# A first convolution by seven products of blocks, and the normed last batch finished by accumulating loads

## The chip, the core and the metric

The kernel runs on one core of a Trainium2 chip. The core has a matrix engine (TensorE, PE in the profile; PEld is its weight load), VectorE (DVE), ScalarE (ACT), GpSimd (POOL), and SyncE (SP), which here does nothing but issue DMA transfers. The metric is the time of one execution on the device in microseconds, the median of several. All arrays are float32.

## What is computed

The reference takes x of shape (4, 1024, 32, 32), so B = 4 batches of C = 1024 channels and N = 1024 tokens, through two layers.

```
layer 0 (attention, per batch; tokens x channels):
  q, k, v = split(x @ w_qkv.T + b_qkv)          # 16 heads of 64
  q, k = rmsnorm(rope(q)), rmsnorm(rope(k))     # over all 1024 channels
  ctx = softmax(q k^T / 8) v
  x1 = rmsnorm(ctx @ w_proj.T) * norm_out_w + x
layer 1 (bottleneck, over all four batches together):
  h1 = relu(bn(conv1x1(x1, w1) + b1))           # 1024 -> 256 channels
  h2 = relu(bn(conv3x3(h1, w2) + b2))           # 256 -> 256
  h3 = bn(conv1x1(h2, w3) + b3)                 # 256 -> 1024
  out = relu(x1 + softplus(residual_scale) * h3)
```

A batch norm (bn) needs the mean and variance of a channel over all four batches, so no part of h1 can be used before the first convolution is done for every batch. The change lies in that convolution and in the end of layer 0 for the last batch.

## The kernel before

`program` (line 86) goes through the batches in order. For each one it projects q, k and v, turns and norms q and k, does the attention head pair by head pair, and projects the result (`qk_proj` with the tag "y", line 1087). The tiles are 128 channels (partitions) by 512 tokens, half a batch; N = 1024 tokens are two such halves (`half`, line 180), 1024 channels are NT = 8 tiles.

The big projections already use products of blocks. A matrix product in which both operands are cut in 2 x 2 blocks is done with seven block products instead of eight, after Strassen in Winograd's form: operand blocks are added and subtracted first (VectorE: `sums` at line 271 for the rows, `operands` at line 224 for the weights, where the four sums are called S1 to S4), and the products are added up in two PSUM banks, one of which is read out several times while it accumulates (`project`, lines 321 to 361). `project2` (line 432) does this on two levels for the later batches. The first convolution does not: `conv1` (line 847) accumulates eight matmuls (1024 input channels in eight tiles) for one of two blocks of 128 output channels and one half of the tokens. That is 4 x 8 = 32 matmuls of 128x512 a batch.

The result y of the last projection of a batch is scaled by the reciprocal root of its mean square. `inverse_rms` (line 657) sums squares over channels with a small matmul (`ss_y`, line 666), takes the root (ScalarE), the reciprocal (VectorE), stores that row to DRAM and broadcasts it to all partitions, both from GpSimd's queue (lines 676 and 677). For batches 0 to 2, `o_norm` then scales y and stores it to `x1d` in DRAM; the input x is added there later by accumulating DMA transfers (line 1037). For the last batch, `last_norm` (line 830) does it in 16 half tiles: VectorE scales, VectorE adds x, which was loaded into the tile `xr` (line 1098), and SP stores to `x1d` (line 837). y stays in SBUF, because the first convolution of batch 3 reads it from there.

After the last projection stand the first convolutions, from line 1094: batch 1 from `back[1]`, batch 2 from `back[2]`, batch 0 from `back[0]`, all read back from `x1d`, and batch 3 from y (line 1194). `back[1]` is read during the last projection (line 1080). `back[0]` takes the place of `back[1]` and so can only be loaded when batch 1 is done. Each result h goes through ScalarE (bias, PSUM to a temporary), VectorE (`bn_stats` for the batch norm) and SP (store to `h1d`). Batch 3 is last; when its first 128 channels are done, the batch norm is put together and the 3x3 convolution begins.

Order of the work: TensorE, GpSimd, VectorE and ScalarE run their instructions in the order in which the program records them (`manual_schedule`, lines 91 and 964). An instruction that waits holds up all that is recorded behind it on its engine. `product_done` (line 252) counts the products; with `after(n, step)` a step is recorded n products later, with `waiting` when the count allows. SP's queue is ordered by a planner when the kernel is built. SBUF is full: the temporaries (`temp`, four of 128x512), the large ones (`big_temp`, three), eight weight chunks (`chunk`) and the large tiles "v", "q", "x" and "k" are handed on from use to use, and a new user waits until the old one is done.

Of the kernel before, what the change touches and what calls it, by code (L numbers as in the profile page):

```python
# [12 lines left out]
AF = mybir.ActivationFunctionType  # L13
ALU = mybir.AluOpType
# [4 lines left out]
P = 128  # L19
B, C, H, W = 4, 1024, 32, 32  # L20
N = H * W
NT = C // P
HD = 64
NHP = C // (2 * HD)
CH = 512
NCH = N // CH
# [3 lines left out]
NPT = PL // P  # L30
# [31 lines left out]
NH = NT // 2  # L62
NG = NT // 2
QH = P // 4
SUMS = ("S2", "S1", "S3", "S4")
# [20 lines left out]
def program(ctx, tc, x, wblk, w2, w3, vecs, cos, sin, out, bad):  # L86


    nc = tc.nc
# [6 lines left out]
    x1d = dram.tile([NT, P, B * N], F32, name=f"x1d{u}")  # L96
    h1d = dram.tile([NPT, P, B * N], F32, name=f"h1d{u}")
# [13 lines left out]
    def col(name, i=0):  # L111
        return vec[:, COL[name] + i : COL[name] + i + 1]
# [30 lines left out]
    h1stats = const.tile([P, NPT, B * NCH, nc.vector.BN_STATS_DIM], F32, name="h1stats")  # L143
# [9 lines left out]
    with tc.tile_pool(name=f"st{u}", bufs=2) as st, ExitStack() as s:  # L153
# [25 lines left out]
        yt = {}  # L179
        half = [slice(c * CH, (c + 1) * CH) for c in range(NCH)]  # L180
# [17 lines left out]
        def bank(kind, name):  # L198
            pool, shape = psum[kind]
            return pool.tile(shape, F32, tag=kind, name=name)  # L200

        def temp(name):
            return tmp.tile([P, CH], F32, tag="tmp", name=name)

        def big_temp(name):
            return big.tile([P, N], F32, tag="big", name=name)
# [5 lines left out]
        def chunk(name):  # L212
            return wring.tile([P, NH, P], F32, tag="w", name=name)
# [28 lines left out]
        TT = 0.21  # L242
        later, waiting = [], deque()
# [5 lines left out]
        def after(n, step):  # L249
            later.append((pace["at"] + n, step))  # L250

        def product_done(share=1.0):
            pace["at"] += share
            pace["room"] = min(pace["room"] + share, 1.2)
            due = [s for at, s in later if at <= pace["at"]]
            later[:] = [(at, s) for at, s in later if at > pace["at"]]
            for step in due:
                step()
            while waiting and pace["room"] > 0 and not pace["hold"]:
                next_waiting()  # L260

        def next_waiting():
            cost, step = waiting.popleft()
            spend(cost)
            step()
# [561 lines left out]

            inverse_rms(total, eps_rms, 1.0 / C, f"y_{b}", then)

        def last_norm(b, total, ys, xr):  # L830


            def norm(f, at):
                y = ys[:, f, at]
                nc.vector.scalar_tensor_tensor(y, y, col("ow", f), total[:, at], ALU.mult, ALU.mult)
                nc.vector.tensor_tensor(y, y, xr[:, f, at], ALU.add)
                nc.sync.dma_start(x1d[f, :, b * N + at.start : b * N + at.stop], y)

            def then():
                waiting.extend([(2 * TT, lambda f=f, at=at: norm(f, at)) for at in half for f in range(NT)])  # L840

            inverse_rms(total, eps_rms, 1.0 / C, f"y_{b}", then)

        def conv1_weights(name):
            return [[block(W1, f, ih, f"c1_{name}_{f}_{ih}") for ih in range(2)] for f in range(NPT)]

        def conv1(b, f, c, w, ys, then=None):
            o = bank("o2", f"c1_{b}_{c}_{f}")
            for i in range(NT):
                ih, ii = divmod(i, NH)  # L850
                nc.tensor.matmul(  # L851
                    o, w[f][ih][:, ii, :], ys[:, i, half[c]], start=(i == 0), stop=(i == NT - 1)
                )
                if i == NH - 1:
                    product_done()
            h = temp(f"h1_{b}_{c}_{f}")
            nc.scalar.activation(h, o, AF.Identity, bias=col("b1", f))

            def stats():
                nc.vector.bn_stats(h1stats[:, f, b * NCH + c, :], h)  # L860
                nc.sync.dma_start(h1d[f, :, b * N + c * CH : b * N + (c + 1) * CH], h)
                if then is not None:
                    then()

            after(1, stats)
            product_done()

        def norm_of(stats, g, be, name):
# [48 lines left out]
        def read_back(b, rows=range(NT)):  # L917
            for i in rows:
                nc.sync.dma_start(back[b][:, i, :], x1d[i, :, b * N : (b + 1) * N])

        def x_tile(b):
            return xp.tile([P, NT, N], F32, tag="x", name=f"x_{b}")
# [4 lines left out]
        def v_room(name):  # L927
            return kv.tile([P, N // P, C], F32, tag="v", name=name)
# [47 lines left out]
        room = v_room("rq_0")  # L976
        for b in range(B):
# [69 lines left out]
            room = v_room(f"to_{b}")  # L1047
# [12 lines left out]
            if b + 1 < B:  # L1060
                xs[b + 1] = x_tile(b + 1)
                ts[b + 1] = t_tiles(b + 1)
                rows = (0, 1, 4, 5, 2, 3, 6, 7)
                for j in range(NT):

                    def load(b=b, i=rows[j]):
                        for c in range(NCH):
                            load_x(b + 1, c, (i,))

                    after(3 + 1.5 * j, load)  # L1070
                for i in range(0, NH, 2):

                    def queue(b=b, i=i):
                        waiting.append((7 * TT, lambda: sums(ts[b + 1], xs[b + 1], i)))

                    after(3 + 1.5 * (2 * i + 3) + 2, queue)
            else:
                back = {1: x_tile(b + 1)}
                for i in range(NT):
                    after(8 + 1.5 * i, lambda i=i: read_back(1, (i,)))  # L1080
            if b == 0:
                weight_parts([parts_of[WK][k] for k in (2, 3)], 6, 7, 4, pieces_of(room[:, 3 * NT // 4 :, :]))
            yt[b] = kp.tile([P, NT, N], F32, tag="k", name=f"y_{b}")
# [3 lines left out]
            ty = qk_proj(b, WP, q_all, tc_, None, yt[b], "y", None, two)  # L1087
            if b + 1 < B:
                o_norm(b, ty, yt[b])
            else:  # L1090
                xr = v_room("xr")
                last_norm(b, ty, yt[b], xr)

        back[2] = kv.tile([P, NT, N], F32, tag="q", name="back")
        read_back(2)
        w = conv1_weights("last")
        for i in range(NT):
            nc.sync.dma_start(xr[:, i, :], x[B - 1, i * P : (i + 1) * P, :])
        for b in (1, 2, 0):
            if b == 0:  # L1100
                back[0] = x_tile("back")
                read_back(0)
            for c in range(NCH):
                for f in range(NPT):
                    conv1(b, f, c, w, back[b])
        rest()
        if bad is not None:
            dt = temp("dens")
# [169 lines left out]
        for b in range(B):  # L1278
            steps = []
            if b + 1 < B:  # L1280
                steps = transform(b + 1, 0) + transform(b + 1, 1)
# [5 lines left out]
            for f in range(NPT):  # L1287
                for h in range(2):
# [14 lines left out]
                    steps = steps[4:]  # L1303
# [9 lines left out]
            if b == 0 and bad is not None:  # L1313
                o = ps.tile([P, CH], F32, tag="mm", name="fit")
# [20 lines left out]
        for f in range(NT):  # L1335
            if f > 0 and f + 2 < NT:
                load_x1(f + 2)
            stats = st.tile([P, B * NCH, nc.vector.BN_STATS_DIM], F32, tag="s3", name=f"s3_{f}")
# [5 lines left out]
            for i, k in order:  # L1344
                b, c = divmod(i, NCH)
                nc.tensor.matmul(  # L1346
                    os[i], w3t[k][f // NH][:, f % NH, :], h2[b, k][:, half[c]],
                    start=(k == 0), stop=(k == NPT - 1),
# [3 lines left out]
                h = h3s[f % 2][:, b, half[c]]  # L1352
# [89 lines left out]
```

## Time and profile before

| | |
|---|---|
| median of 3 runs | 2709.47 us (2709.33 to 2710.42) |
| the profiled execution | 2709.99 us, span 2708.2 us |
| TensorE busy in the span | 2669.3 us, 99% |
| VectorE, ScalarE, GpSimd busy | 2169.5, 1096.1 and 452.6 us |
| mean granted clock of TensorE | 0.995 |
| moved from and to HBM | 316.71 MB read, 96.78 MB written |

The span runs from the first to the last instruction; the execution's time has a little around it. Times inside the trace count from the start of the span. "Waits" of an engine are idle times and what ended them. The clock is the share of full speed that was granted to TensorE. A matmul of the source appears as two records[...]. Records overlap, so a matmul's cost is read from start to start.

### The profile page before, as it was taken

What the parts mean: (1) busy time and instruction counts of PE and PEld (TensorE: products, weight loads), DVE (VectorE), ACT (ScalarE), POOL (GpSimd) and SP (SyncE); (2) the same over time, 40 slices, a digit from 0 to 9 for tenths busy, and PEclk for the clock granted to TensorE, in tenths of its full rate; (3) what the DMA queues carried; (4) which work ended last, traced back from release to release, by engine and by line L of the source; (5) the groups of instructions that cost most, each with busy time, mean ns of one, the idle gap of its engine ahead of it and who ended that gap; (6) DMA issues with size and microseconds to landing.
All of it is one profiled execution on the core that took longest, in us unless ns stands there. A gap on an engine that the chain in (4) does not pass through costs nothing. (4 is left out here: it accounts for less than half of the span.)

```text
span 2708.2 us, 32563 instructions
## 1 busy us (share of the span) xinstructions
PE 2669.3 (99%) x11410; PEld 1659.0 (61%) x11410; DVE 2169.5 (80%) x2516; ACT 1096.1 (40%) x1520; POOL 452.6 (17%) x552
## 2 busy tenths in 40 slices
PE   9999999999999999999999999999999999999997
PEld 4448533488888333688886333888884335746843
DVE  4577899998887977888878877987888878646987
ACT  2222455523342555333343555233525553312266
POOL 2562222322011211100111211100111211000000
PEclk9999999999999999999999999999999999999999
DMA  7897755587677341456765420665783314662165
GB/s 272 317 306 214 230 154 165 167 269 246 197 203 213 62 92 32 148 152 222 188 189 144 88 54 17 214 205 173 189 233 79 75 36 132 196 240 86 63 227 209
DMA packets 245964, 453.54 MB, mean 167 GB/s; under 512 B 28384, under 2 KB 117264, under 8 KB 245792
## 3 DMA queue, kind: packets, MB, share of 16 engines
q1 hardware_dynamic: 203568, 310.72, 36.5%
q0 software_dynamic: 42224, 140.63, 19.6%
q8 instruction: 94, 1.54, 0.2%
q14 instruction: 78, 0.64, 0.1%
HBM read 316.71 MB, written 96.78 MB: 153 GB/s over the span
## 5 line engine op out<-in xcount | busy, mean ns | idle before, releaser
L768 DVE TENSOR_TENSOR den<-den,p 128x1024 f32<-128x1024 f32 x384 | 470.5, 1225 | 40.7 <-DVE den L768 0.9
L764 ACT ACTIVATE p<-sc 128x1024 f32<-128x1024 f32 x512 | 476.3, 1043 | 55.0 <-PE sc L757 54.8
L757 PE MATMUL sc<-q,k 64*128 64x512 f32 x2048 | 457.7, 596 | 0.0
L757 PEld LDWEIGHTS sc<-q,k 64*128 64x128 f32 x2048 | 189.9, 186 | 265.6 <-issue 121.2
L774 PE MATMUL cx<-p,to 128*64 128x512 f32 x1536 | 340.2, 595 | 0.0
L774 PEld LDWEIGHTS cx<-p,to 128*64 128x64 f32 x1536 | 106.0, 137 | 228.3 <-issue 228.3
L738 POOL TENSOR_SCALAR q<-q,vec 128x512 f32<-128x512 f32 x64 | 127.0, 1989 | 559.2 <-DVE q L737 559.2
L453 PE MATMUL p_v<-w_v,x 128*128 128x256 f32 x928 | 210.8, 380 | 1.3 <-DVE x L424 1.3
L458 PE MATMUL p_y<-q,w_y 128*128 128x256 f32 x928 | 210.1, 380 | 1.1 <-DMA w_y<-wdf 1.1
L458 PEld LDWEIGHTS p_y<-q,w_y 128*128 128x128 f32 x928 | 175.9, 190 | 28.5 <-issue 4.8
L453 PEld LDWEIGHTS p_v<-w_v,x 128*128 128x128 f32 x928 | 176.9, 191 | 26.8 <-DVE x L424 2.1
L779 ACT COPY q<-cx 128x512 f32<-128x512 f32 x64 | 37.5, 587 | 356.9 <-PE cx L774 356.9
L458 PE MATMUL p_k<-to,w_k 128*128 128x256 f32 x672 | 154.8, 384 | 4.7 <-ACT to L547 4.7
L458 PE MATMUL p_q<-to,w_q 128*128 128x256 f32 x672 | 152.5, 380 | 0.7 <-ACT q L512 0.6
L458 PEld LDWEIGHTS p_k<-to,w_k 128*128 128x128 f32 x672 | 127.9, 192 | 26.3 <-ACT to L547 7.1
L458 PEld LDWEIGHTS p_q<-to,w_q 128*128 128x128 f32 x672 | 127.2, 190 | 20.2 <-ACT q L512 1.9
L766 DVE TENSOR_TENSOR den<-p 128x1024 f32<-128x1024 f32 x64 | 76.5, 1195 | 77.3 <-ACT p L764 77.3
L806 DVE RECIPROCAL rec<-dn 128x512 f32<-128x512 f32 x32 | 107.2, 3352 | 20.6 <-PE dn L800 20.6
L774 PE MATMUL cx<-p,rq 128*64 128x512 f32 x512 | 113.4, 595 | 0.0
L1346 PE MATMUL c<-h,w 128*128 128x512 f32 x256 | 110.3, 592 | 0.9 <-ACT h L1248 0.9
L700 POOL DMA_DIRECT2D k<-ks x64 | 56.1, 1036 | 278.2 <-ACT p L764 111.0
L453 PE MATMUL p_v<-w_v,t 128*128 128x256 f32 x384 | 92.0, 385 | 3.6 <-DMA w_v<-in_wblk_dram 3.6
(444 smaller groups left out, 4188.0 us busy)
## 6 DMA issues: line engine op xcount, KB each, us to landing
w_v<-wd2f SPq DMA_DIRECT2D x112, 256.0 KB
w_y<-wd2f SPq DMA_DIRECT2D x112, 256.0 KB
w_q<-wd2f SPq DMA_DIRECT2D x84, 256.0 KB
w_k<-wd2f SPq DMA_DIRECT2D x84, 256.0 KB
x<-in_x_dram SPq DMA_DIRECT2D x64, 256.0 KB
q<-qs POOLq DMA_DIRECT2D x64, 256.0 KB, 5.7
k<-ks POOLq DMA_DIRECT2D x64, 256.0 KB, 4.5
inv<-rec SPq DMA_DIRECT2D x256, 64.0 KB
```

The source lines that it names most:

```text
L453: nc.tensor.matmul(o[:, q].rearrange("p (g f) -> p g f", g=2), r[:, i, q * P : (q + 1) * P], wt[:, :, i, :], skip_group_check=True, **at,)
L458: nc.tensor.matmul(o[:, q], wt[:, q, i, :], r[:, i, :], skip_group_check=True, **at)
L700: nc.gpsimd.dma_start(dst[i::2, f, :], other[1 - i :: 2, :], accum_op=ALU.add)
L738: nc.gpsimd.tensor_scalar(cx, cx, col("bv", hp), None, ALU.add)
L757: nc.tensor.matmul(sc[:, j], k_all[d, hp, t * P : (t + 1) * P], q_all[d, hp, at], start=True, stop=bad is not None,)
L764: nc.scalar.activation(p, sc, AF.Exp)
L766: nc.vector.tensor_tensor(d_, probs[0], p, ALU.add)
L768: nc.vector.tensor_tensor(d_, d_, p, ALU.add)
L774: nc.tensor.matmul(o[j * HD : (j + 1) * HD, :], v[:, t, h0 : h0 + HD], probs[t][:, j], start=(t == 0), stop=(t == N // P - 1),)
L779: nc.scalar.copy(q_all[:, hp, at], o)
L806: nc.vector.reciprocal(r, dn)
L1346: nc.tensor.matmul(os[i], w3t[k][f // NH][:, f % NH, :], h2[b, k][:, half[c]], start=(k == 0), stop=(k == NPT - 1),)
```

## The change

The three batches 1, 2 and 0 are now done by seven products of blocks. The left operand is w1 cut in two blocks of output channels and two of input channels (a11, a12, a21, a22, each four tiles of 128x128), the right one is the batch cut in two blocks of channels and two halves of tokens (b11, b12, b21, b22). `conv1_sums` makes S1 to S4 of the weights once. `t_sums` makes the sums of the rows of a batch; it overwrites b12 and b21, and for batches 2 and 0 also b11. `four` is one product, four matmuls. `conv1_first` does the two products that need no sums and `conv1_rest` the other five, in turn on two banks, with a `yield` after each of the first four. The loop at the end starts the next batch's first two products and row sums after two of the five.

For batch 1 three of the four row sums are recorded during the last projection (`first_sums`), into a free part of `room` and into `big_temp` tiles; the rows of `back[1]` are read back earlier and in another order. `last_norm` now scales whole tiles; x is added to them by accumulating DMA transfers from GpSimd's queue into SBUF, and after the eighth, eight stores to `x1d` follow on the same queue. `xr` is gone; `back[0]` is loaded into its place (tile "v") as soon as that is free, instead of into that of batch 1. Batch 3 is computed as before.

```diff
--- before.py
+++ after.py
@@ -827,17 +827,19 @@
 
             inverse_rms(total, eps_rms, 1.0 / C, f"y_{b}", then)
 
-        def last_norm(b, total, ys, xr):
-
-
-            def norm(f, at):
-                y = ys[:, f, at]
-                nc.vector.scalar_tensor_tensor(y, y, col("ow", f), total[:, at], ALU.mult, ALU.mult)
-                nc.vector.tensor_tensor(y, y, xr[:, f, at], ALU.add)
-                nc.sync.dma_start(x1d[f, :, b * N + at.start : b * N + at.stop], y)
+        def last_norm(b, total, ys):
+
+
+            def norm(f):
+                y = ys[:, f, :]
+                nc.vector.scalar_tensor_tensor(y, y, col("ow", f), total, ALU.mult, ALU.mult)
+                nc.gpsimd.dma_start(y, x[b, f * P : (f + 1) * P, :], accum_op=ALU.add)
+                if f == NT - 1:
+                    for i in range(NT):
+                        nc.gpsimd.dma_start(x1d[i, :, b * N : (b + 1) * N], ys[:, i, :])
 
             def then():
-                waiting.extend([(2 * TT, lambda f=f, at=at: norm(f, at)) for at in half for f in range(NT)])
+                waiting.extend([(2 * TT, lambda f=f: norm(f)) for f in range(NT)])
 
             inverse_rms(total, eps_rms, 1.0 / C, f"y_{b}", then)
 
@@ -856,13 +858,99 @@
             h = temp(f"h1_{b}_{c}_{f}")
             nc.scalar.activation(h, o, AF.Identity, bias=col("b1", f))
 
-            def stats():
-                nc.vector.bn_stats(h1stats[:, f, b * NCH + c, :], h)
-                nc.sync.dma_start(h1d[f, :, b * N + c * CH : b * N + (c + 1) * CH], h)
+            def done():
+                keep_h1(b, f, c, h)
                 if then is not None:
                     then()
 
-            after(1, stats)
+            after(1, done)
+            product_done()
+
+        def keep_h1(b, f, c, h):
+            nc.vector.bn_stats(h1stats[:, f, b * NCH + c, :], h)
+            nc.sync.dma_start(h1d[f, :, b * N + c * CH : b * N + (c + 1) * CH], h)
+
+        def conv1_sums(w):
+
+            (a11, a12), (a21, a22) = w
+            s2, s1, s3, s4 = (chunk(f"c1_{o}") for o in SUMS)
+            nc.vector.tensor_tensor(s1, a21, a22, ALU.add)
+            nc.vector.tensor_tensor(s2, s1, a11, ALU.subtract)
+            nc.vector.tensor_tensor(s3, a11, a21, ALU.subtract)
+            nc.vector.tensor_tensor(s4, a12, s2, ALU.subtract)
+            return s2, s1, s3, s4
+
+        def t_sums(ys, t1, t2, i, steps=range(4)):
+
+            at, low = slice(i, i + 2), slice(i + NH, i + NH + 2)
+            b11, b12, b21, b22 = (ys[:, r, h] for r in (at, low) for h in half)
+            for out, p, q in [(t1, b12, b11), (t2, b22, t1), (b12, b22, b12), (b21, b21, t2)][steps[0] : steps[-1] + 1]:
+                nc.vector.tensor_tensor(out, p, q, ALU.subtract)
+
+        mine = {}
+
+        def four(o, wt, rows, first, last):
+            for i in range(NH):
+                nc.tensor.matmul(
+                    o, wt[:, i, :], rows(i), start=first and i == 0, stop=last and i == NH - 1,
+                    skip_group_check=True,
+                )
+
+        def conv1_first(b, ys, w):
+
+            o = mine[b] = bank("o1", f"c1_{b}")
+            four(o, w[0][0], lambda i: ys[:, i, half[0]], True, False)
+            h = temp(f"c11_{b}")
+            nc.scalar.copy(h, o)
+            product_done()
+            o2 = bank("o2", f"c1a_{b}")
+            four(o2, w[0][1], lambda i: ys[:, i + NH, half[0]], True, True)
+
+            def done():
+                nc.vector.scalar_tensor_tensor(h, o2, col("b1", 0), h, ALU.add, ALU.add)
+                keep_h1(b, 0, 0, h)
+
+            after(1, done)
+            product_done()
+
+        def conv1_rest(b, ys, w, ss, t1, t2):
+
+            o = mine[b]
+            four(o, ss[0], t2, False, False)
+            h12 = temp(f"c12_{b}")
+            nc.scalar.copy(h12, o)
+            product_done()
+            yield
+            o2 = bank("o2", f"c1s_{b}")
+            four(o2, ss[1], t1, True, False)
+            p5 = temp(f"c1p_{b}")
+            nc.scalar.activation(p5, o2, AF.Identity, bias=col("b1", 1))
+            product_done()
+            yield
+            four(o, ss[2], lambda i: ys[:, i, half[1]], False, False)
+            h22 = temp(f"c22_{b}")
+            nc.scalar.copy(h22, o)
+
+            def done22():
+                nc.vector.tensor_tensor(h22, h22, p5, ALU.add)
+                keep_h1(b, 1, 1, h22)
+
+            after(1, done22)
+            product_done()
+            yield
+            four(o2, ss[3], lambda i: ys[:, i + NH, half[1]], False, True)
+
+            def done12():
+                nc.vector.scalar_tensor_tensor(h12, o2, col("b1", 0), h12, ALU.add, ALU.add)
+                keep_h1(b, 0, 1, h12)
+
+            after(1, done12)
+            product_done()
+            yield
+            four(o, w[1][1], lambda i: ys[:, i + NH, half[0]], False, True)
+            h21 = temp(f"c21_{b}")
+            nc.scalar.activation(h21, o, AF.Identity, bias=col("b1", 1))
+            after(1, lambda: keep_h1(b, 1, 0, h21))
             product_done()
 
         def norm_of(stats, g, be, name):
@@ -1075,9 +1163,19 @@
 
                     after(3 + 1.5 * (2 * i + 3) + 2, queue)
             else:
+
                 back = {1: x_tile(b + 1)}
-                for i in range(NT):
-                    after(8 + 1.5 * i, lambda i=i: read_back(1, (i,)))
+                for j, i in enumerate((0, 1, 4, 5, 2, 3, 6, 7)):
+                    after(3 + 1.5 * j, lambda i=i: read_back(1, (i,)))
+                t1 = room[:, 3 * NT // 4 :, :].rearrange("p a (c t) -> p (a c) t", c=NCH)
+                t2 = {}
+
+                def first_sums(i):
+                    t2[i] = big_temp(f"t2_1_{i}").rearrange("p (a t) -> p a t", a=2)
+                    t_sums(back[1], t1[:, i : i + 2, :], t2[i], i, range(3))
+
+                for i in range(0, NH, 2):
+                    after(14 + 3 * i, lambda i=i: waiting.append((5 * TT, lambda: first_sums(i))))
             if b == 0:
                 weight_parts([parts_of[WK][k] for k in (2, 3)], 6, 7, 4, pieces_of(room[:, 3 * NT // 4 :, :]))
             yt[b] = kp.tile([P, NT, N], F32, tag="k", name=f"y_{b}")
@@ -1088,21 +1186,34 @@
             if b + 1 < B:
                 o_norm(b, ty, yt[b])
             else:
-                xr = v_room("xr")
-                last_norm(b, ty, yt[b], xr)
-
+                last_norm(b, ty, yt[b])
+
+        w = conv1_weights("last")
         back[2] = kv.tile([P, NT, N], F32, tag="q", name="back")
         read_back(2)
-        w = conv1_weights("last")
-        for i in range(NT):
-            nc.sync.dma_start(xr[:, i, :], x[B - 1, i * P : (i + 1) * P, :])
-        for b in (1, 2, 0):
-            if b == 0:
-                back[0] = x_tile("back")
-                read_back(0)
-            for c in range(NCH):
-                for f in range(NPT):
-                    conv1(b, f, c, w, back[b])
+        back[0] = v_room("back")
+        read_back(0)
+        conv1_first(1, back[1], w)
+        ss = conv1_sums(w)
+        for i in range(0, NH, 2):
+            t_sums(back[1], None, t2[i], i, range(3, 4))
+        room1, sums2 = t1, t2
+        rows1, rows2 = (lambda i: room1[:, i, :]), (lambda i: sums2[i // 2 * 2][:, i % 2, :])
+        for b, nxt in ((1, 2), (2, 0), (0, None)):
+            steps = conv1_rest(b, back[b], w, ss, rows1, rows2)
+            for _ in range(2):
+                next(steps)
+            if nxt is not None:
+                ys, new = back[nxt], {}
+                conv1_first(nxt, ys, w)
+                for i in range(0, NH, 2):
+                    new[i] = big_temp(f"t2_{nxt}_{i}").rearrange("p (a t) -> p a t", a=2)
+                    t_sums(ys, ys[:, i : i + 2, half[0]], new[i], i)
+            for _ in steps:
+                pass
+            if nxt is not None:
+                rows1 = lambda i, ys=ys: ys[:, i, half[0]]
+                rows2 = lambda i, new=new: new[i // 2 * 2][:, i % 2, :]
         rest()
         if bad is not None:
             dt = temp("dens")
```

## The prediction

> **What bounds the kernel now.** I read the page's busy shares first, then one window over the stage that the diff rewrites, then the rows of its matmuls, then TensorE's list of waits.
>
> ```profile
> PE 2669.3 (99%) x11410; PEld 1659.0 (61%) x11410; DVE 2169.5 (80%) x2516; ACT 1096.1 (40%) x1520; POOL 452.6 (17%) x552
> ...
> PEclk9999999999999999999999999999999999999999
> ```
>
> TensorE (PE) is busy for 99% of the span of 2708.2 us. So a matmul that goes away is worth its own length, and any new idle time of TensorE is lost in full. The window from the first matmul of the first convolution to the first one of batch 3 says the same of this stage (fields after the window: its length, then busy us of PE, PEld, DVE, ACT, POOL, the granted clock, DMA share, GB/s):
>
> ```profile
> 2357.00:2440.00 83.00, 83.00 (x201) 36.58 (x201) 35.72 (x52) 11.39 (x17) 3.26 (x4) 1.00 0.70 249
> ```
>
> TensorE never rests here, VectorE (DVE) works 36 of 83 us. The rows of line 851 give the price of a matmul (durations, then first and last start):
>
> ```profile
> L851 PE MATMUL c<-back,w_c_last x64: 592/592/592, 2385.3 to 2412.3; 128*128 128x512 f32 x64
> ...
> L851 PE MATMUL c<-x_back,w_c_last x64: 592/592/593, 2412.7 to 2439.8; 128*128 128x512 f32 x64
> ...
> L851 PE MATMUL c<-y,w_c_last x64: 592/592/592, 2440.2 to 2467.3; 128*128 128x512 f32 x64
> ```
>
> A batch is 32 matmuls of the source and 64 records, and takes (2440.2 - 2385.3)/2 = 27.45 us, so one matmul of the source costs 27.45/32 = 0.858 us start to start (the 592 ns overlap), and four of them, one product of the new scheme, 3.43 us.
>
> **The change, part by part.**
>
> *Seven products.* Batches 1, 2 and 0 need 7 x 4 = 28 matmuls each instead of 32: 12 fewer, 12 x 0.858 = 10.3 us off TensorE.
>
> *The first S2 product.* This is where I see a new stall. VectorE runs its instructions in written order. For batch 1 the order after A12 is: add the A12 bank into h (new L910, waits for the end of A12), bn_stats of it, then S1, then S2 of the weights. TensorE needs S2 right after A12. A11 and A12 are the eight matmuls that in the trace run from 2357.05; their successor could start 8 x 0.858 later, at 2363.9, and the first reader of those eight (ScalarE, L857) starts at 2364.11. The spacing of such a VectorE sequence, start to start, stands here:
>
> ```profile
> 2386.20 0.69 DVE L860 BATCH_NORM_STATS2 h1stats<-h 128x6 f32<-128x512 f32 x1 [6.17 <-ACT h L857]
> 2386.81 0.73 DVE L835 SCALAR_TENSOR_TENSOR y<-y,vec,sqy 128x512 f32<-128x512 f32 x1
> 2387.58 0.69 DVE L836 TENSOR_TENSOR y<-y,xr 128x512 f32<-128x512 f32 x1
> ```
>
> 0.61 us to an instruction that doesn't depend on the one before, 0.77 after a scalar_tensor_tensor to one that does. An earlier stage shows the same situation, weight sums made while TensorE waits for S2 (L233):
>
> ```profile
> 184.94 0.68 DVE L231 TENSOR_TENSOR w_k_3b_s<-w_k_3b,w_k_3b 128x512 f32<-128x512 f32 x1
> ...
> 185.66 0.69 DVE L232 TENSOR_TENSOR w_k_3b<-w_k_3b,w_k_3b 128x512 f32<-128x512 f32 x1
> ...
> 186.38 0.69 DVE L233 TENSOR_TENSOR w_k_3b<-w_k_3b_s,w_k_3b 128x512 f32<-128x512 f32 x1
> ...
> 187.13 2.12 PE L298 MATMUL pa_k<-t,w_k_3b 128*128 128x512 f32 x3 [1.99 <-DVE w_k_3b L233]
> ```
>
> Dependent sums follow at 0.72 us, and TensorE starts 0.06 us after S2 ends. So: 2364.11 + 0.77 (to bn_stats) + 0.61 (to S1) + 0.72 (to S2) + 0.69 (S2 itself) + 0.06 = 2366.96, against 2363.9. **Stall: 3.0 us.** Nothing hides it, for everything on TensorE behind that product waits too.
>
> *What the gap does to the clock.* The waits of TensorE in the whole trace (total, times, longest):
>
> ```profile
> PE p_k L458 <- ACT to L547: 4.7, 6, 2.4
> PE p_v L453 <- DMA w_v<-in_wblk_dram: 3.6, 1, 3.6
> PE pa_k L298 <- DVE w_k_3b L233: 2.0, 1, 2.0
> ...
> PE c2x L1205 <- DVE V L1145: 1.5, 2, 1.0
> PE p_v L453 <- DVE x L424: 1.3, 2, 1.2
> ```
>
> and windows just after the 2.0 us and the 3.6 us gap, and two later (same fields; the third number from the end is the clock):
>
> ```profile
> 187.00:188.00 1.00, 0.87 (x2) 0.49 (x3) 0.97 (x3) 0.00 (x0) 0.53 (x1) 0.99 1.02 397
> 188.00:189.00 1.00, 1.00 (x2) 0.33 (x1) 1.00 (x3) 0.56 (x1) 0.40 (x1) 0.50 1.03 406
> 282.00:283.00 1.00, 1.00 (x4) 0.82 (x3) 1.00 (x3) 0.59 (x1) 0.00 (x0) 0.50 1.04 404
> 286.00:288.00 2.00, 2.00 (x11) 1.77 (x10) 1.97 (x4) 0.00 (x0) 0.00 (x0) 1.00 0.66 208
> ```
>
> After each of the three gaps of 2.0, 2.4 and 3.6 us TensorE ran at half clock for a while; after gaps of 1.2 us and less it did not. What that took, from matmul starts: after 2.0 us, eight records in 5.23 us (187.13 to 192.36) where the same form takes 3.43, so 1.8 us; after 2.4 us, 32 records in 8.70 instead of 6.90, 1.8 us; after 3.6 us, 16 records in 6.14 instead of 3.45, 2.7 us. [...] The rows say that 2.0 us was enough, so I charge it. Bounds: 0[...] to 2.7; I take 1.8, what both shorter gaps cost.
>
> *VectorE's other new work.* Sums of rows: 24 of 128x1024 at 1.22 us = 29.3 us; weight sums 4 x 0.69 = 2.8; nine adds of banks at 0.69 to 0.74 = 6.5. Gone: 16 scalings and 16 additions of 0.742 and 0.691 = 22.9, for eight scalings of 1.28 (the row of L822) = 10.2. Net +26 us, of which 7.3 (the first six row sums) lie in the projection: one trio starts at about 2320.6, where it delays later adds by some 0.1 us before VectorE's 1.61 us idle at 2327.9 takes it up, the other fills an idle 3.46 us at 2349.8. Cost 0. In the stage itself VectorE reaches about 55 of 78 us. TensorE waits for it at two more places, S2 of batches 2 and 0: after A12 ends VectorE needs 0.2 + 0.77 + 0.61 and six sums (4.68 for the first four, then 1.27 + 1.23), 8.8 us in all, and TensorE has S3, S4 and A22 of the batch before to do, 10.3 us, and 1.7 us more until it reads the second half. Slack 3.2 us; cost 0. Without that cover each us of lateness is a us of time. Before batch 0, VectorE must also have finished the eight scalings; they wait for the broadcast of the rms row, due by about 2392 (landing 4.1 to 5.6 us after issue), and VectorE gets to them at about 2397.
>
> *Two banks in turn.* The ScalarE copy that each accumulating product waits for (0.2 + 0.59 us) lies under a product of the other bank, 3.43 us. Cost 0; it would be 0.8 us a time.
>
> *Queues.* SP loses eight 512 KB loads (xr) and 16 stores; the loads of batch 2 start at 2358.9 as before and no longer share with xr (4.2 MB at the 361 GB/s seen from 2360 to 2370 is 11.6 us, landed by 2371, needed at about 2376). The loads of batch 0 now wait on SP for the S1 product of batch 1, about 2375, and land by 2388, needed at 2400; the h1 stores queue behind them. Their temporaries pass to later copies: the tightest have about 4 to 8 us for a landing that a 256 KB store makes in 3.5 to 6.7 (the landings of x1d stores). POOL gains eight accumulating loads (issue 0.82 to 1.75 us, the row of L700) and eight stores (0.53 us, L823); behind them stand only the two memsets of pad (1.06 each), wanted 17 us after batch 3 starts. The last scaling ends near 2408, an accumulating 512 KB transfer landed in 8.0 us, at most 14.3 (L1037), so y is whole by about 2422, and batch 3 starts near 2434.7. Cost 0.
>
> **The sum.** 10.3 - 3.0 - 1.8 = 5.5 us less. Against the profiled execution, 2709.99 us (span 2708.2 and 1.8 around it), that is 2704.5; the median of the runs, 2709.47, is 0.5 below that execution, so the median after is 2704.0. Own range of this case: 2703 to 2705.
>
> **Rivals.**
> *The clock stays full*[...]: 2709.5 - 7.3 = 2702.2. For it, gaps up to 1.2 us left it full; against it, the three rows above. 0.17.
> *Another wait on top.* The copy of c22 in batch 1 takes the temporary of the rms row, so it waits for that row's store on POOL: reciprocal done near 2380, issue 0.6, landing 1.7 to 5.1, so 2382.6 to 2386; it is needed by 2389. Landing in 10 us would stop A22 by about 2 us, with another 1.8 for the clock. Such a wait, here, at the loads or at a temporary: 2705 to 2709. 0.17.
> *Slower.* The eight accumulating loads of y don't overlap. They start near 2398; batch 3 must wait for all of them, and the gain is used up at 2440.2, that is at 42/8 = 5.3 us a load one after another. At 6 us each: 2715. Against: eight 512 KB stores in a row (L823) landed within 9.0 us. 0.06.
> That the products don't go away is no case: the instructions are written out.
>
> **How the numbers follow.** The likeliest case has 0.60 and gives 2704.0. I take 0.2% (5.4 us, 2704.05) as what a measurement of this kernel can tell from no change. The likeliest case straddles that line: slightly over half of its 0.60, 0.33, falls below, and with the 0.17 of the full clock faster has 0.50; the rest of it and the extra wait make 0.44 for same; slower 0.06. The range 2701.6 to 2707.5 takes in the full clock with 0.6 us to spare and the smaller half of the extra waits; outside are their larger half and the slower case, under 0.2.
>
> **What would show it.** Right: the new matmul rows of batches 1, 2, 0 hold 168 records; one wait of TensorE, about 2.9 us, at the S2 product of batch 1, released by VectorE's L878; a clock of 0.50 within 3.4 us of it; no wait at S2 of batches 2 and 0; batch 3's first matmul near 2434.7, and the rest of the trace shifted as it is. Wrong: that gap with the clock at 1.00; waits of TensorE for ScalarE's copies or for DMA in this stage; a wait of batch 3's first matmuls for the loads into y.

## The result and the profile after

The median went from 2706.26 us (13 runs) to 2700.72 us (13 runs): the ratio is 0.9977, with an interval of 0.9970 to 0.9984, so 5.5 us less. Measured again later beside two other kernels, it was 2702.44 (21 runs) against 2706.63 (27 runs): 0.9983, interval 0.9977 to 0.9990, 4.2 us less. The forecast gain of 5.5 us was met; that the first measurement hits it to the tenth is luck, since its interval reaches from 4.3 to 8.1 us. The forecast time of 2704.0 us was not met: 2700.72 lies below the range of 2701.6 to 2707.5, because the kernel before takes 2706.3 us in the median and not the 2709.5 of its first three runs.

The page of the changed kernel has this for TensorE (busy us, share of the span, instructions), where 2669.3 us stood before:

```profile
span 2697.9 us, 32539 instructions
...
PE 2656.7 (98%) x11386; PEld 1652.7 (61%) x11386; DVE 2194.8 (81%) x2529; ACT 1097.2 (41%) x1523; POOL 461.2 (17%) x568
```

The busy time fell by 12.6 us. The two profiled spans differ by 10.3 us, and only about half of that is the change's. The first convolution, from its first matmul to the first of the 3x3 convolution, took 110.63 us before and 105.33 after: 5.3 us. What follows took the same within 0.1 us. The other 5.1 us were won ahead of the stage, in instructions that the change doesn't touch (the first matmul started at 2357.05 before, at 2351.96 after). Ahead of the stage the trace before has four stretches of 3.4 us at half clock, this one has one.

TensorE's waits between 2340 and 2480 us, of which the kernel before has none, are one line in the changed kernel (total, times, longest):

```profile
PE c L894 <- DVE c_S L878: 3.1, 1, 3.1
```

The order of time around it, VectorE first, then TensorE (start, duration, instruction, idle time before it and what ended that):

```profile
2359.11 0.75 DVE L910 SCALAR_TENSOR_TENSOR c<-c1a,vec,c 128x512 f32<-128x512 f32 x1 [4.84 <-PE c1a L894]
2359.90 0.69 DVE L870 BATCH_NORM_STATS2 h1stats<-c 128x6 f32<-128x512 f32 x1
2360.51 0.67 DVE L877 TENSOR_TENSOR c_S<-w_c_last,w_c_last 128x512 f32<-128x512 f32 x1
2361.22 0.69 DVE L878 TENSOR_TENSOR c_S<-c_S,w_c_last 128x512 f32<-128x512 f32 x1
...
2351.96 3.60 PE L894 MATMUL c<-x,w_c_last 128*128 128x512 f32 x8
2355.40 3.60 PE L894 MATMUL c1a<-x,w_c_last 128*128 128x512 f32 x8
2362.05 5.37 PE L894 MATMUL c<-t,c_S 128*128 128x512 f32 x8 [3.06 <-DVE c_S L878]
2367.26 3.60 PE L894 MATMUL c1s<-to,c_S 128*128 128x512 f32 x8
```

This is the chain of the prediction: add, statistics, S1, S2, and TensorE behind them. A product is 3.44 us here (2351.96 to 2355.40), so S2 could have started at 2358.84: it is 3.2 us late. It then took 5.21 us to the next product, 1.78 too many. The windows around it show the clock at 0.50 (length, busy us of PE, PEld, DVE, ACT, POOL, granted clock, DMA share, GB/s):

```profile
2352.00:2430.00 78.00, 74.94 (x178) 32.65 (x177) 53.12 (x59) 12.67 (x20) 12.44 (x18) 0.98 0.82 257
2359.40:2362.80 3.40, 0.75 (x2) 0.49 (x3) 3.33 (x6) 0.00 (x0) 0.00 (x0) 1.00 1.01 399
2362.80:2366.20 3.40, 3.40 (x5) 1.35 (x4) 3.29 (x5) 0.18 (x1) 0.00 (x0) 0.50 1.00 382
2366.20:2369.00 2.80, 2.80 (x8) 1.17 (x7) 1.97 (x3) 1.04 (x2) 0.00 (x0) 1.00 0.32 124
```

In the window up to 2362.8 TensorE is busy for 0.75 of 3.40 us; in the next one it works without a pause at half clock. Between 20 and 2600 us the stretches at half clock begin at 277.24 and 2362.78 us in this trace, 611 x 3.4133 us apart, and at 187.98, 276.73 and 785.31 us in the trace before, 26 and 149 x 3.4133 us apart; each lasts 3.413 us, the one at 276.73 twice that. So the traces are cut below into pieces of 3.413 us from these starts. Such a piece is called a window of the clock, the series of its edges the grid of that trace.

### The profile page after: what moved, and what is told of

Its sections match the earlier page's. It is cut to its first block, busy times and chain, and to the rows that moved or that the text cites. A ratio compares the mean times of both kernels' runs of the same rounds, so it can differ in the third digit from the quotient of the medians.

```text
span 2697.9 us, 32539 instructions
## 1 busy us (share of the span) xinstructions
PE 2656.7 (98%) x11386; PEld 1652.7 (61%) x11386; DVE 2194.8 (81%) x2529; ACT 1097.2 (41%) x1523; POOL 461.2 (17%) x568
```

## The experiments

**Take the stall away.** In the first experiment the four weight sums go between the first two products of batch 1, where VectorE is idle for 4.84 us.

```diff
-        def conv1_first(b, ys, w):
+        def conv1_first(b, ys, w, mid=lambda: None):
...
             nc.scalar.copy(h, o)
             product_done()
+            mid()
             o2 = bank("o2", f"c1a_{b}")
...
-        conv1_first(1, back[1], w)
-        ss = conv1_sums(w)
+        ss = []
+        conv1_first(1, back[1], w, lambda: ss.extend(conv1_sums(w)))
```

> The changed kernel with the four sums of the weights recorded between the first two products of batch 1 (A11 and A12) instead of behind the add and the statistics of A12. VectorE is idle for 4.84 us there. My theory: the stall at the S2 product (3.2 us from start to start) goes, and with it the window at half clock that followed it (1.8 us), so 5.0 us less than the changed kernel, which is 10.5 us less than the kernel before (5.5 + 5.0); no wait of TensorE for c_S, no clock of 0.50 in the stage. Rival, the clock drop there had another cause: the stall goes, the half clock stays: 3.2 us less than the changed kernel, 8.7 less than the kernel before. Rival, the rows of batch 2 or a temporary are late next, now that TensorE asks for them 5 us sooner: 5.5 to 8 us less than the kernel before, with a new wait of TensorE for DMA or ScalarE in the stage.

Measured: 2696.30 us in the median (5 runs), 0.9957 of the kernel before (0.9944 to 0.9970), 9.8 us less where I had put 10.5. The stage took 100.44 us, 4.9 less than in the changed kernel and 10.2 less than before. Its order of time (TensorE, then VectorE):

```profile
2356.87 3.60 PE L894 MATMUL c<-x,w_c_last 128*128 128x512 f32 x8
2360.30 3.60 PE L894 MATMUL c1a<-x,w_c_last 128*128 128x512 f32 x8
2363.73 3.60 PE L894 MATMUL c<-t,c_S 128*128 128x512 f32 x8
2367.17 3.60 PE L894 MATMUL c1s<-to,c_S 128*128 128x512 f32 x8
...
2359.80 0.69 DVE L878 TENSOR_TENSOR c_S<-c_S,w_c_last 128x512 f32<-128x512 f32 x1
...
2364.01 0.75 DVE L911 SCALAR_TENSOR_TENSOR c<-c1a,vec,c 128x512 f32<-128x512 f32 x1 [2.31 <-PE c1a L894]
```

S2 of the weights is done 3.2 us before TensorE asks for it, the products follow without a gap, and TensorE waits for nothing in the stage, at a clock of 1.00. So the whole gain of the 12 removed matmuls (10.3 us by the prediction) is there once the stall and its window are gone. No other wait took their place.

**Fill the gap, keep the stall.** Here S2 comes as late as before, but TensorE is kept busy.

```diff
         conv1_first(1, back[1], w)
+        warm = bank("o2", "warm")
+        for i in range(3):
+            nc.tensor.matmul(warm, w[1][1][:, i, :], back[1][:, i + NH, half[0]], start=True, stop=True)
         ss = conv1_sums(w)
```

> The changed kernel with three matmuls of no use (2.6 us, into a bank that nobody reads) between A12 and S2 of batch 1, where TensorE waits 3.1 us for the sums. S2 starts as late as in the changed kernel, but TensorE is idle for only some 0.6 us. My theory, idle time costs 1.8 us of clock on top of the stall: S2's eight records take 3.43 us instead of 5.21, and the kernel is 1.8 us faster than the changed one, 7.3 us faster than the kernel before. Rival, the half clock behind the gap was chance or costs nothing in the end: as the changed kernel, 5.5 us faster than the kernel before.

Measured: 2698.56 us (10 runs), ratio 0.9970 (0.9961 to 0.9979), 7.6 us under the kernel before; the stage took 103.63 us, 1.7 less than in the changed kernel.

```profile
2357.88 2.74 PE L1199 MATMUL warm<-x,w_c_last 128*128 128x512 f32 x6
2361.11 3.67 PE L894 MATMUL c<-t,c_S 128*128 128x512 f32 x8 [0.49 <-DVE c_S L878]
2364.61 3.60 PE L894 MATMUL c1s<-to,c_S 128*128 128x512 f32 x8
```

S2's product is as late (10.10 us after the first one of the stage, 10.09 in the changed kernel), but now it takes 3.50 us instead of 5.21. Three matmuls of no use made the stage shorter: what they saved is the clock. That the grid happened to lie well here is no explanation: an edge of this trace's grid is at 2360.49 us, so without them the idle time from 2358.05 to 2361.11 would have filled 0.71 of one window, and in the count below half clock followed each of the 22 idle times that filled 0.59 or more. The medians alone would not show it, for the interval of this ratio overlaps those of the changed kernel.

**The end of layer 0 alone.** The new `last_norm`, with the first convolution as before.

```diff
-        def last_norm(b, total, ys, xr):
+        def last_norm(b, total, ys):
...
-                nc.vector.tensor_tensor(y, y, xr[:, f, at], ALU.add)
-                nc.sync.dma_start(x1d[f, :, b * N + at.start : b * N + at.stop], y)
+                nc.gpsimd.dma_start(y, x[b, f * P : (f + 1) * P, :], accum_op=ALU.add)
...
-        for i in range(NT):
-            nc.sync.dma_start(xr[:, i, :], x[B - 1, i * P : (i + 1) * P, :])
```

> The kernel before with one part of the change alone: last_norm scales whole tiles, x is added by accumulating loads from GpSimd's queue, eight stores follow there, and the loads of x into xr are gone. The first convolution stays at 32 matmuls a batch. My theory: this part costs and brings nothing, since TensorE waits for neither VectorE nor these transfers before batch 3: within 1 us of the kernel before. Rival, a part of the gain is its (12.7 us less of VectorE, 24 transfers less on SP): 1 to 3 us faster. Rival, batch 3 waits for the accumulating loads: slower by 1 us or more, with a wait of the first matmuls that read y.

Measured: 2707.37 us (14 runs), ratio 1.0004 (0.9995 to 1.0012), and a stage of 110.63 us, to the hundredth that of the kernel before. In this stage this part neither costs nor brings anything; the runs alone leave room for 1.4 us won to 3.2 us lost.

**The order of the products.**

```diff
             four(o, ss[0], t2, False, False)
...
+            four(o, ss[2], lambda i: ys[:, i, half[1]], False, False)
+            h22 = temp(f"c22_{b}")
+            nc.scalar.copy(h22, o)
+            product_done()
+            yield
             o2 = bank("o2", f"c1s_{b}")
             four(o2, ss[1], t1, True, False)
...
-            four(o, ss[2], lambda i: ys[:, i, half[1]], False, False)
-            h22 = temp(f"c22_{b}")
-            nc.scalar.copy(h22, o)
```

> The changed kernel with the products of one bank behind each other once a batch: S2, S3, S1, S4, A22 instead of S2, S1, S3, S4, A22. S3 adds to the bank that ScalarE is still copying after S2. My step: 0.8 us a time (0.2 until the copy starts and 0.59 for it), three times, so 2.4 us more in the stage, 107.7 us where the changed kernel takes 105.3 from the first matmul of the first convolution to the first one of the 3x3; three waits of TensorE for ScalarE's copy; no clock of 0.50 from them. Rival, the accumulation into the bank does not have to wait or is hidden: 105.3.

Measured: one run, 2705.44 us, with a stage of 110.70 us where I had put 107.7. I had overlooked that this order puts S1 and S4, which share the other bank, behind each other as well, so there are six waits and not three.

```profile
2362.40 3.67 PE L894 MATMUL c<-t,c_S 128*128 128x512 f32 x8 [3.06 <-DVE c_S L878]
2367.86 3.70 PE L894 MATMUL c<-x,c_S 128*128 128x512 f32 x8 [1.79 <-ACT c L921]
...
2379.03 3.60 PE L894 MATMUL c1s<-to,c_S 128*128 128x512 f32 x8
2383.41 3.70 PE L894 MATMUL c1s<-x,c_S 128*128 128x512 f32 x8 [0.78 <-ACT c1p L932]
2386.94 3.60 PE L894 MATMUL c<-x,w_c_last 128*128 128x512 f32 x8
2390.38 3.60 PE L894 MATMUL c<-t,c_S 128*128 128x512 f32 x8
2394.65 3.70 PE L894 MATMUL c<-back,c_S 128*128 128x512 f32 x8 [0.68 <-ACT c L921]
```

From start to start a wait for a plain copy cost 4.27 - 3.43 = 0.84 us, one for a copy with bias 4.38 - 3.43 = 0.95, and the product after each took 0.1 more: about 1.0 us a time, where I had put 0.8. The first of the six cost 2.0, since ScalarE still had a square to do (2366.37 to 2367.00) that waits for VectorE. Five waits of about 1.0 and one of 2.0 are 7 us, and the stage is 7.1 us longer than the 103.6 that it takes at full clock with the stall. Taking the two banks in turn avoids these; the mechanism was right.

The same trace shows something that matters more. The gap at S2 is 3.06 us, exactly that of the changed kernel, but here the product behind it takes its usual time, and the clock stays full:

```profile
2357.80:2361.20 3.40, 1.54 (x4) 0.38 (x2) 1.71 (x3) 0.30 (x1) 0.00 (x0) 1.00 1.02 404
2361.20:2364.60 3.40, 2.20 (x5) 1.06 (x6) 3.37 (x6) 0.00 (x0) 0.00 (x0) 1.00 1.06 401
2364.60:2368.00 3.40, 1.61 (x5) 0.52 (x4) 3.12 (x4) 1.22 (x2) 0.00 (x0) 1.00 0.79 307
```

An edge between two windows falls into the gap at 2361.2: they are idle for 1.86 and 1.20 of 3.40 us and the clock stays at 1.00, where in the changed kernel one window was idle for 2.65 and the next had 0.50.

**The same program again.** This asks why executions of one kernel differ.

> The kernel before once more, for a second trace of the same program. Theory C, read from the six traces so far: [...] a window in which TensorE was idle for more than 0.60 of it puts the next at half clock, one idle for less than 0.50 does not (between them both were seen). So the same idle times of 2.0 to 3.6 us cost 1.7 us in one execution and nothing in the next; this execution has one to three such windows, not always the four of the first trace, each followed by the rule from its grid. The rest of the difference to the first trace is waits for transfers and for VectorE in the projections of q, k, v and y; the attention, the first convolution (110.63 us from its first matmul to that of the 3x3) and what follows take the same to 0.1 us. Theory D, the idle time alone decides (2.0 us and more always costs 1.8): the same three places at half clock as in the first trace.

> The kernel before, a third trace. As for the second: by theory C the places at half clock differ from those of the other two traces, and each window follows the rule of its idle share; by theory D they are the same three.

Measured: 2704.77 us and 2709.07 us, where the first trace had 2709.99. An edge of the grid lies at 188.0 us in the first trace and at 189.3 us in the second. First the windows of the first trace of the kernel before, cut on its grid at the three early gaps, then those of the second (2704.77 us) on its own, taken from its last change at 2691.3:

```profile
184.60:188.00 3.40, 1.41 (x4) 0.49 (x3) 3.30 (x6) 1.32 (x2) 1.44 (x2) 1.00 1.04 326
188.00:191.40 3.40, 3.40 (x5) 1.33 (x4) 1.66 (x3) 1.26 (x2) 1.66 (x3) 0.50 1.04 383
273.30:276.70 3.40, 1.39 (x7) 0.89 (x5) 3.33 (x6) 0.88 (x2) 1.73 (x4) 1.00 1.11 284
276.70:280.10 3.40, 1.82 (x4) 1.51 (x5) 3.40 (x4) 0.00 (x0) 3.37 (x5) 0.50 1.02 373
280.10:283.50 3.40, 3.40 (x9) 2.70 (x8) 3.18 (x5) 0.59 (x1) 0.00 (x0) 0.50 1.04 407
781.90:785.30 3.40, 1.05 (x6) 0.74 (x5) 2.85 (x5) 2.46 (x5) 0.00 (x0) 1.00 0.52 151
785.30:788.70 3.40, 3.40 (x10) 2.69 (x9) 3.31 (x6) 0.00 (x0) 0.00 (x0) 0.50 0.11 8
```

And the second trace, same fields:

```profile
185.90:189.30 3.40, 1.86 (x5) 0.91 (x6) 3.30 (x7) 1.56 (x3) 1.56 (x4) 1.00 0.99 366
189.30:192.70 3.40, 3.40 (x10) 1.49 (x9) 0.67 (x2) 1.29 (x3) 1.46 (x3) 1.00 1.05 374
274.70:278.10 3.40, 2.00 (x9) 1.80 (x10) 3.40 (x4) 0.00 (x0) 3.10 (x5) 1.00 1.03 362
278.10:281.50 3.40, 3.40 (x17) 2.99 (x17) 3.37 (x6) 1.17 (x2) 0.00 (x0) 1.00 1.05 415
779.80:783.20 3.40, 2.07 (x10) 1.84 (x11) 2.83 (x5) 1.24 (x3) 0.00 (x0) 1.00 0.28 80
783.20:786.60 3.40, 3.40 (x17) 3.01 (x16) 3.29 (x7) 0.59 (x1) 0.00 (x0) 1.00 0.47 105
```

The idle times are nearly the same (2.0, 3.6 and 2.4 us; 1.9, 2.8 and 2.4 us). The first execution has four windows at half clock, the second has none. The third again had four, at the same places, and took 2709.07. My expectation of one to three windows, at other places, was wrong both times; but of the windows at full clock above, those idle for 1.99 to 2.35 us of 3.40 were followed by half clock, those idle for 1.33 to 1.54 us, or not at all, were not. The third trace alone would also have suited theory D; the second rules it out. I then took every idle time of TensorE of 1.4 us or more between 20 and 2600 us in 13 traces, 42 in all, with the largest share of a window on that trace's grid that it fills:

| largest idle share of a window of 3.413 us | idle times | next window at half clock |
|---|---|---|
| up to 0.54 | 15 | 0 |
| 0.55 to 0.58 | 5 | 3 |
| 0.59 and more | 22 | 22 |

An idle time of 3.06 us is in the first row (share 0.54) and in the last (0.78 and 0.79): in these traces not its length decided, but how much of one window it filled. The gap of 2.35 us near 782 us shows it too: 0.69 of one window in the trace before, and half clock follows; 0.50 and 0.19 of two windows in the changed kernel, and the clock stays full.

**Matmuls of no use in the three early gaps.** The kernel before, with this in three places:

```diff
+                if tag == "k" and b == 0 and g == 3:
+                    nc.tensor.matmul(bank("o2", "fill_a"), w[4][:, 0, :], right["A22"](0), start=True, stop=True)
                 product(o, w[0], "S2", False, False)
...
+                if tag == "v" and b == 0 and k == 6:
+                    for _ in range(2):
+                        mm(bank2("o2", "fill_v"), w[5][4], t_[5][2], True, True)
...
+                if tag == "k" and b == 1 and k == 5:
+                    mm(bank2("o2", "fill_k"), w[k][6], t_[k][3], True, True)
                 mm(o, w[k][6], t_[k][3], False, True)
```

> The kernel before with matmuls of no use (into banks that nobody reads) in the three early idle times of TensorE: one of 0.86 us before the S2 product that waits for the last weight sums of k of batch 0, eight of 0.43 us before the product of v of batch 0 that waits 3.6 us for its weights, four of 0.43 us before the product of k of batch 1 that waits 2.4 us for ScalarE. What those products wait for is not changed. Theory A, the runs of one kernel differ by how many idle times meet a window of the clock: no window at half clock is left there (the profiled execution of the kernel before had four, 6.8 us), the median falls by 3 to 5 us to about 2702, and the runs lie within 3 us of each other where those of the kernel before lie 8 apart. Theory B, the runs differ by something else (transfers, say): the median moves by less than 1 us and the spread stays.

Measured: 2705.55 us (13 runs), ratio 0.9997 (0.9989 to 1.0006). The mean granted clock rose from 0.9968 to 0.9976 and the standard deviation of the runs fell from 2.6 to 1.8 us, so the windows at half clock are part of the spread; but the median fell by 0.6 us and not by 3 to 5. With early sums, and one product instead of two in the middle place:

> The changed kernel with the sums of the weights between A11 and A12 (as in the run with early sums), and with matmuls of no use in the three early idle times of TensorE, this time with only one product (1.7 us) before the one that waits 3 us or more for its weights, so that at most 1.9 us stay idle there. Theory C: none of the three places idles for 0.60 of a window, so the 1.7 us that each costs in some executions are gone; from the mean clock of the runs with early sums (0.997, some 1.5 windows more than with no loss at those places) that is 1.5 to 2.5 us less than those, a median of about 2694, 12 us under the kernel before. Rival: as in the run of the kernel before with such matmuls, nothing above 1 us is won, the median stays at 2696, and what moves the runs lies in the waits for transfers.

Measured: 2695.30 us (6 runs), ratio 0.9948 (0.9936 to 0.9961), between the two forecasts. To compare the versions on one chip, I ran three once more together:

> The changed kernel once more, beside the next two on one chip. By its stage it stands 5.3 us under the kernel before where the 3.1 us gap at S2 idles TensorE for over 0.6 of a window of the clock, and 7.0 where the gap straddles two windows: 5.5 us under it in the median. The stage, from the first matmul of the first convolution to the 3x3 convolution, takes 105.3 us with such a window and 103.6 without; nothing between.

> The changed kernel with early sums, once more: a stage of 100.4 us, in the median 4.5 to 5 us under the changed kernel on the same chip.

> Early sums and the matmuls of no use at the three early idle times, once more. Theory C: no window at half clock at these three, and 1 to 2.5 us under the kernel with early sums on the same chip, with runs that lie closer together. Rival: the same within 0.5 us, since the waits for transfers and for VectorE in the other projections (batch 3's v among them) set as much of the spread.

Measured: the changed kernel 2702.44 (ratio given above; its stage took 105.13 us: its gap idles 0.78 of a window and half clock follows, but the first 0.39 us of that window still lie in the gap, so it costs 1.5 us and not 1.7), early sums 2696.33 (5 runs, 0.9956, interval 0.9943 to 0.9969), early sums with fillers 2698.96 (6 runs, 0.9961, interval 0.9947 to 0.9975). Early sums stand, 6.1 us under the changed kernel here, where I had put 4.5 to 5. The fillers show no gain on top of them, which is nearer to the rival; with six runs 9 us apart it says no more. The traces show one place where a gain of theirs can go. In all three with fillers the v projection of batch 3 took 89.4 to 90.0 us, in the other ten 86.4 to 87.6. From one of the three (VectorE, then TensorE):

```profile
1998.22 1.23 DVE L694 TENSOR_TENSOR sinT<-sinT,sqk 128x1024 f32<-128x1024 f32 x1 [6.88 <-DMA sinT<-in_sin_dram]
...
2002.48 4.00 PE L455 MATMUL p_v<-w_v,x 128*128 128x256 f32 x10 [2.08 <-DVE x L426]
```

VectorE is held up by the load of a rotation table, TensorE by the row sums behind it, and in these three traces a window at half clock follows. Why that wait is longer with fillers (2.0 to 2.6 us against 0.6 to 1.8) I have not settled; SyncE issues its transfers in the same order with and without them.

## Where the prediction failed, and what in it was right

The time failed at its anchor, the baseline that the gain was taken from; the gain held. Part by part, with the anchor last:

*Seven products, 10.3 us: right.* With the stall gone, the stage is 10.2 us shorter.

*The stall of 3.0 us: right*, measured 3.2. Every row of its chain came in the order forecast, with spacings within 0.1 us of it.

*The clock, 1.8 us: the size was right, the rule was not.* One window cost 1.7 us (filled gap) to 1.8 (order of time). But I read from three rows that "2.0 us was enough" and charged it as fixed; the gap at S2 was followed by half clock in both traces of the changed kernel and not in the trace with another order of products. The rival of a full clock, with 10.3 - 3.0 = 7.3 us less, is therefore no other case but another throw of the same dice: behind a gap of 3.06 us the clock stayed at 1.00 in one trace, where the gap filled at most 0.54 of a window, and fell to 0.50 in two, where it filled 0.79 and 0.78. Half clock followed each of the 22 idle times that filled 0.59 or more. If a gap can fall anywhere on the grid, which is assumed here and not shown, the chance to escape for a length g between 2.0 and 4.0 us is about (4.0 - g)/3.413, an estimate from these 0.59 on both sides of an edge and the windows of 3.413 us: 0.28 at 3.06 us. The price to charge was some 0.72 x 1.7 = 1.2 us on average, and a little less where the window at half clock begins in the gap.

*VectorE's slack before S2 of batch 2, 3.2 us: right.* The second half of its rows was done at 2387.12 and needed at 2390.34. *The end of layer 0, at no cost: right*, by the experiment; y was whole when the last store could be issued, at 2418.59, and batch 3 starts at 2429.82.

*The other rivals did not come.* The copy of c22 in batch 1, which takes the rms row's temporary, waited for TensorE alone (2381.96), and batch 3 started 11 us after y was whole. *But the landing of the h1 stores was mis-sized:* I gave the tightest temporaries 4 to 8 us for one of 3.5 to 6.7 us, and it took longer. From ScalarE's order of time in the changed kernel:

```profile
2421.72 0.69 ACT L927 ACTIVATE c1p<-c1s,vec 128x512 f32<-128x512 f32 x1 [4.84 <-DMA h1df<-c]
```

This copy of batch 0 waits for the store that frees its temporary, issued 7.7 us before at 2413.93. It ends at 2422.41, and TensorE needs its bank at 2422.96: 0.55 us to spare. Two other stores of h1 that ScalarE waited for took 9.1 and 9.7 us. They run beside the accumulating loads, whose landing took 10.6 us in the median and at most 15.5, where I had taken 8.0 and 14.3; that these loads slow the stores is likely, not shown.

*The step that failed is the anchor of the sum*: "the median of the runs, 2709.47, is 0.5 below that execution, so the median after is 2704.0". Three runs within 1.1 us of each other were taken for the kernel's time, and the range allowed for the change's unknowns alone. All 83 runs of the kernel before, from every comparison, lie between 2702.1 and 2713.7 us, with a median of 2706.4; 18 of them are at 2709.33 or more. If runs were independent, three in a row from there would come about once in a hundred times; whether the first three shared a cause, beyond what follows, the record doesn't show. Of 70 the granted clock is recorded:

| mean granted clock | runs | mean time, us |
|---|---|---|
| 0.998 | 7 | 2703.9 |
| 0.997 | 39 | 2705.9 |
| 0.996 | 19 | 2709.8 |
| 0.995 | 5 | 2711.7 |

One window at half clock lowers the mean by 0.5 x 3.413/2706 = 0.0006 and costs 1.7 us, so 0.001 should cost 2.7; the rows give 7.8/3 = 2.6. The profile that I read already said so: it had four such windows, 6.8 us, behind gaps that can pass without one. By the estimate above, gaps of 2.0, 2.4 and 3.6 us bring about 0.4, 0.5 and 0.9 windows. Some two fewer than in that execution is 3.4 us less, 2706.6, and with the gain of 5.5, 2701. This fits, but it is worked out after the fact, and with fillers at these three places the median fell by 0.6 us only. It doesn't explain the whole spread either: waits for transfers and for VectorE in the projections, of batches 0 and 1 above all, differ by up to 1.7 us a projection between traces where no window at half clock lies in it, while the attention takes the same to 0.02 us. What sets those waits is open.

## What to carry to other kernels

Before adding a gain to a baseline, look for windows at half clock in the profiled execution and ask which of them the next execution will have; three runs that agree don't say. Price a gap on TensorE by its own length plus the chance that it fills 0.59 of one window (half clock in 22 of 22 cases here), times the 1.7 us that one such window cost here. A gap of at most 1.85 us (0.54 of a window) had only its length here; three of 1.9 to 2.0 us still brought a window at half clock. And where a new operand is made on an engine that runs its instructions in the order recorded, as VectorE did here (add, statistics, S1 and S2 from 2359.11 to 2361.91 us), record it ahead of work that waits for the engine it feeds: that one move took 4.9 us off the stage, nearly as much again as the change's 5.3.

## What was not expected of the hardware

Idle times of 2.35 us at one place passed at full clock in three traces and brought a window at half clock in six, in programs that are the same up to there. Three extra matmuls in a gap shortened a stage by 1.7 us. And windows at half clock that were themselves partly idle were followed by different clocks: with 0.46 and 0.23 of the window idle (the first and third trace of the kernel before, at 276.7 and 277.4 us) the clock stayed at 0.50 for a second window, with 0.11 (at 2360.7, the changed kernel's second trace) it was back at 1.00.
